# Two 256x256 float32 layers rewritten as three reduced-precision products each, with their tables moved to make room

## The chip, the cores and the metric

The kernel runs on one core of one Trainium2 chip. The metric is the device time of one execution in microseconds (us); three executions of the kernel before gave 1525.33, 1526.73 and 1530.22 us, median 1526.73.

A core has five engines with one in-order queue each: TensorE (PE in the profile; its weight loads are listed as PEld), VectorE (DVE), ScalarE (ACT), GpSimd (POOL) and SyncE (SP, which here only issues DMAs).

## The reference, cut to what matters

The program is a chain of four residual layers on x of shape 4 x 1024 x 256: a linear recurrence with a small network behind it, a sparse feed-forward layer, attention, and the feed-forward layer again. The change touches the first one only:

```python
u = einsum('btd,edh->ebth', x, W_in) + b_in          # three 256x256 layers
in_r, in_i, o = u
h = scan(lam * h + gamma * (in_r + 1j * in_i))        # along the 1024 tokens
out = h.real @ W_mid[0] - h.imag @ W_mid[1] + b_mid[0] - b_mid[1] + o
y = gelu(out @ w1_w + w1_b)                           # first square layer
y = y @ w2_w + w2_b + out                             # second square layer
return layer_norm(y) * ln_g + ln_b                    # added to x
```

The input x is layer-normalized on the way in. The two square layers, 256 x 256 each, are applied to all 4096 tokens.

## The kernel before, in words

**Tiling.** The 4096 tokens lie in 8 blocks of 512; a batch row of 1024 tokens is two blocks, the even and the odd tokens (`CH = 2`), so that one step of the recurrence covers two tokens. Features lie on partitions in two halves of 128 (`KD = 2`, indices `c` for the output half and `k` for the input half). Everything up to about 298 us is this layer plus the heads (normalize, transpose, small convolution) of the feed-forward layer behind it; then come the feed-forward tiles, the attention (the longest stage) and the second feed-forward layer.

**Steps of a block.** `Lru.head` (L357) normalizes and transposes a block of x and splits it into a high and a low part (`xnt`, type float32r). `Lru.states` (L381) makes the inputs of the recurrence on TensorE (tile `pu`), evacuates them on ScalarE (L390), rotates them by tables of cosines and sines `ct`, `st` on VectorE (L402 to L407), scans (L410) and rotates back (L411 to L416). `Lru.outputs` (L422) makes `po` on TensorE (L432 and L437), evacuates it with its bias into `ot` on ScalarE (L438), multiplies by the first square matrix in float32 (L443, tile `pz`), applies Gelu into `zt` (L446), multiplies by the second (L452), adds bias and `ot` on VectorE (L455), transposes (L465), normalizes and adds to x: `yn` on ScalarE (L474), three adds or products on GpSimd (L482 to L484). `Ffn.head` (L501) then takes the finished x.

**Two kinds of product.** The float32 products are single `matmul` calls on float32 tiles. The split products (`products`, L165) take three float32r matmuls for one product of two matrices: high by high, high by low, low by high.

**Tables.** `Lru.tables` (L230) builds `ct` and `st` by doubling, each one tile of 128 x 2 x 512 in the pool of the layer. `Ffn.head` keeps the convolution's output of block b in tiles `xc0` to `xc7` (L507) of the pool `ffn_b`.

**What sets the order.** The body (from L1075) lists the work block by block; a block's `outputs` is followed by the `states` of a later batch row (blocks 2 to 5 only), by the head of a block four further on and by the head of the feed-forward layer two behind. A scheduler then orders each engine's queue by its own timing model, so the queues interleave neighbouring steps; at run time an instruction that waits holds up all that stands behind it on its engine. Two places are pinned by hand: `issue_after(lru.evacuated[7])` (L1095) puts the loads of x blocks 4 to 7 and of the feed-forward weights behind the eighth evacuation of `states` in ScalarE's queue, and the last block is worked in two halves of 256 tokens (L1117). The weights are loaded from ScalarE's queue as well (L215 to L225).

The two calls of the square layers:

```python
            for k in range(KD):
                nc.tensor.matmul(
                    pz, w[:, k, 2, c * P : (c + 1) * P], ot[:, k, :], start=(k == 0), stop=(k == KD - 1)
                )
```

Of the kernel before, what the change touches and what calls it, by code (L numbers as in the profile page):

```python
# [21 lines left out]
P = 128  # L22
# [157 lines left out]
class Banks:  # L180


    def __init__(self, pool, bufs):
        self.pool, self.bufs = pool, bufs
# [10 lines left out]
class Lru:  # L195
# [2 lines left out]

    def __init__(self, tc, ctx, ident, vecs, brow, w_lru, psum):
        self.tc = tc
        nc = self.nc = tc.nc
        self.ident, self.vecs, self.brow, self.psum = ident, vecs, brow, psum
        cp = ctx.enter_context(tc.tile_pool(name="lru_c", bufs=1))
        self.sp = ctx.enter_context(tc.tile_pool(name="lru_s", bufs=2))
        self.wp = ctx.enter_context(tc.tile_pool(name="lru_w", bufs=1))
        self.cp = cp
        self.evacuated, self.scanned, self.xnt_first = [], [], None
        w = self.w = cp.tile([P, KD, 4, D], F32, tag="w", name="w_lru")  # L210
        wt = self.wt = cp.tile([P, KD, 2, D], F32, tag="wt", name="wt")
        self.w_o = cp.tile([P, KD, D], F32, tag="w_o", name="w_o")

        self.w_in, self.w_mid = {0: [], 1: []}, {1: [[w[:, k, e, :] for e in range(2)] for k in range(KD)]}
        for e in range(3):  # L215
            stage = self.w_o if e == 2 else self.sp.tile([P, KD, D], F32, tag="ot", name="stage")
            nc.scalar.dma_start(stage, w_lru[:, :, e])
            parts = self.two(f"w{e}")
            nc.scalar.copy(parts[0], stage)
            nc.gpsimd.tensor_tensor(parts[1], stage, parts[0].bitcast(F32), ALU.subtract)  # L220
            self.w_in[1].append(parts)
            if e == 1:
                nc.scalar.dma_start(wt, w_lru[:, :, 7:9])
        for e in (slice(3, 5), slice(5, 7)):
            nc.scalar.dma_start(w[:, :, e.start - 3 : e.stop - 3], w_lru[:, :, e])  # L225

    def two(self, name):
        return [self.cp.tile([P, KD, D], F32R, tag=f"{name}{i}", name=f"{name}{i}") for i in range(2)]
# [1 line left out]
    def tables(self, between):  # L230
        nc, cp, vecs = self.nc, self.cp, self.vecs
        par = exp_exact(nc, cp, vecs[:, V_PAR : V_PAR + 6], 6, "par")
        nc.scalar.mul(self.w[:, :, 1, :], self.w[:, :, 1, :], -1.0)

        levels = TC.bit_length()
        ang = cp.tile([P, levels, KD], F32, tag="ang", name="ang")
        powers = cp.tile([P, levels, KD], F32, tag="powers", name="powers")
        for l in range(levels):
            nc.gpsimd.memset(powers[:, l, :], float(2**l))
        nc.vector.tensor_tensor(ang, powers, par[:, None, 2:4].to_broadcast([P, levels, KD]), ALU.mult)  # L240
        cn, sn, self.turns = cos_sin(nc, cp, ang.rearrange("p l c -> p (l c)"), levels * KD)
# [12 lines left out]


        ct = self.ct = cp.tile([P, KD, TC], F32, tag="ct", name="ct")
        st = self.st = cp.tile([P, KD, TC], F32, tag="st", name="st")
        nc.gpsimd.memset(ct[:, :, 0:1], 1.0)
        nc.gpsimd.memset(st[:, :, 0:1], 0.0)
        for l in range(levels - 1):  # L260
            n = 2**l
            for c in range(KD):
                t1 = self.wp.tile([P, 512], F32, tag="u0", name="t1", bufs=4)
                t2 = self.wp.tile([P, 512], F32, tag="u1", name="t2", bufs=4)
                c0, s0 = ct[:, c, 0:n], st[:, c, 0:n]
                c1, s1 = ct[:, c, n : 2 * n], st[:, c, n : 2 * n]
                ca, sa = (v[:, (l + 1) * KD + c : (l + 1) * KD + c + 1] for v in (cn, sn))
                if c == 0:
                    nc.vector.tensor_scalar(t1[:, 0:n], s0, sa, None, ALU.mult)
                    nc.vector.tensor_scalar(t2[:, 0:n], c0, sa, None, ALU.mult)  # L270
                else:
                    nc.scalar.mul(t1[:, 0:n], s0, sa)
                    nc.scalar.mul(t2[:, 0:n], c0, sa)
                nc.vector.scalar_tensor_tensor(c1, c0, ca, t1[:, 0:n], ALU.mult, ALU.subtract)
                nc.vector.scalar_tensor_tensor(s1, s0, ca, t2[:, 0:n], ALU.mult, ALU.add)

    def first_weights(self, lam):
# [1 line left out]
        nc, cp, vecs, wt = self.nc, self.cp, self.vecs, self.wt  # L279
        self.turn = [[lam[:, i, k : k + 1] for i in range(2)] for k in range(KD)]  # L280

        tw = [self.sp.tile([P, KD, D], F32, tag="zt", name=f"tw{e}") for e in range(2)]
# [27 lines left out]
    def output_weights(self):  # L310

        nc, cp, vecs, w, wt = self.nc, self.cp, self.vecs, self.w, self.wt
        gw = [self.sp.tile([P, KD, D], F32, tag="zt", name=f"gw{e}") for e in range(2)]
# [67 lines left out]
    def states(self, xnts, c):  # L381
# [11 lines left out]
            self.evacuated.append(last.ins)  # L393
            u.append(ue)
        ur, ui = u
        cc, ss = self.ct[:, c, :], self.st[:, c, :]
# [20 lines left out]
        return full  # L417

    def buffers(self):
        return [self.sp.tile([P, KD, 512], F32, tag=t, name=t, bufs=n) for t, n in (("ot", 2), ("zt", 2))]  # L420

    def outputs(self, r, xs, xnt, h, pairs, last, tag="po", bufs=None):  # L422

# [4 lines left out]
        ot, zt = bufs or self.buffers()  # L428
        for c in range(KD):
            co = slice(c * P, (c + 1) * P)  # L430
            po = self.psum.tile([P, 512], tag, "po")[:, 0:n]
            self.inputs(po, r, 2, c, xnt, sl, stop=False)  # L432
            terms = [
                (self.w_mid[r][k][e][:, co], h[k][e][:, sl.start + r : sl.stop + r]) for k in range(KD) for e in range(2)
            ]
            for i, (lt, v) in enumerate(terms):
                nc.tensor.matmul(po, lt, v, start=False, stop=(i == len(terms) - 1))  # L437
            nc.scalar.activation(ot[:, c, :], po, AF.Identity, bias=self.ob[:, r, c : c + 1])  # L438
            yield
        for c in range(KD):  # L440
            pz = self.psum.tile([P, 512], "pu", "pz")[:, 0:n]
            for k in range(KD):
                nc.tensor.matmul(  # L443
                    pz, w[:, k, 2, c * P : (c + 1) * P], ot[:, k, :], start=(k == 0), stop=(k == KD - 1)
                )
            last_gelu = nc.scalar.activation(zt[:, c, :], pz, AF.Gelu, bias=vecs[:, V_B1 + c : V_B1 + c + 1])  # L446
        self.last_gelu = last_gelu.ins
        yield
        for c in range(KD):
            pz = self.psum.tile([P, 512], tag, "pz2")[:, 0:n]  # L450
            for k in range(KD):
                nc.tensor.matmul(  # L452
                    pz, w[:, k, 3, c * P : (c + 1) * P], zt[:, k, :], start=(k == 0), stop=(k == KD - 1)
                )
            nc.vector.scalar_tensor_tensor(  # L455
                ot[:, c, :], pz, vecs[:, V_B2 + c : V_B2 + c + 1], ot[:, c, :], ALU.add, ALU.add
            )
# [30 lines left out]
class Ffn:  # L488
# [12 lines left out]
    def head(self, blk, sp, psum, ptag, pairs=(0, 1), xtag="fx", ttag="ft"):  # L501
# [17 lines left out]
        for i, j in enumerate(pairs):  # L519
            r = slice(2 * j, 2 * j + 2)  # L520
            xs = self.x[blk * 4 + 2 * j : blk * 4 + 2 * j + 2]
            pt = normalized_t(nc, sp, psum, xtag, ptag, xs, norm[:, 0, r], norm[:, 1, r], w.ident)
            tt = sp.tile([P, KD, 256], F32, tag=ttag, name="ft", bufs=2 if self.dram else 1)
            nc.scalar.copy(tt, pt)  # L524
            yield
            if self.dram:
# [458 lines left out]
def run(*gens):  # L985
    for g in gens:
        for _ in g:
            pass
# [51 lines left out]
def tile_kernel(ctx: ExitStack, tc: tile.TileContext, x_in, w_lru, vecs_in, rows, w_ffn, lin_t, w_attn, w_down, out):  # L1040
# [34 lines left out]
    with ExitStack() as c1:  # L1075
        psum = Banks(c1.enter_context(tc.tile_pool(name="ps1", space=PSUM)), {"pu": 2, "po": 2, "py": 2, "pt": 2})

        brow = c1.enter_context(tc.tile_pool(name="brow", bufs=1)).tile([P, 2, D], F32, tag="brow", name="brow")
        lru = Lru(tc, c1, ident, vecs, brow, w_lru, psum)
# [33 lines left out]
        for blk in range(4, NBLK - 3):  # L1113
            run(f1.head(blk, lru.sp, psum, "pt"))
        k = NBLK - 1
        ot, zt = lru.buffers()
        halves = [  # L1117
            lru.outputs(k % CH, xb[k], xnt[k], h[k // CH], (i,), last, tag, [v[:, :, c : c + 256] for v in (ot, zt)])
            for i, tag, c in ((0, "pu", 0), (1, "po", 256))
        ]  # L1120
        for i in (0, 0, 1):
# [6 lines left out]
        run(*(f1.head(NBLK - 1, lru.sp, psum, "pu", (i,), "lx", "zt") for i in range(2)))  # L1128

    with ExitStack() as c2:  # L1130
        sp = c2.enter_context(tc.tile_pool(name="at_s", bufs=2))
# [193 lines left out]
```

## Time and profile before

| | us |
|---|---|
| median of the runs shown | 1526.73 |
| the profiled execution | 1528.76 |
| its span, first to last instruction | 1527.0 |
| mean granted TensorE clock, share of full speed | 0.946 |
| first product of the recurrence layer (L170) begins | 22.06 |
| first square layer begins (L443, block 0) | 82.91 |
| last square layer's results transposed (L465) | 274.6 |
| feed-forward logits begin (L556) | 297.9 |

How to read the profile: durations are of one profiled execution. In the view of instructions in order of time a row is start, duration, engine, line, operation, output<-input, shape, and how many were merged; brackets hold the idle time of the engine before it and what released it. In the table of windows, the figures are busy us of each engine in that stretch and the granted TensorE clock. A float32 matmul leaves two records, a float32r matmul one. The ends of matmuls are modelled, so the rate is read from the distance between starts: the duration that a record shows is about 0.16 us longer.

Engines in the stages of this layer (busy us of the stretch):

| stretch, us | length | PE | DVE | ACT | POOL | clock |
|---|---|---|---|---|---|---|
| 82.9 to 93.7, block 0 behind the recurrence | 10.8 | 8.71 | 8.55 | 6.73 | 3.26 | 0.86 |
| 94.1 to 116.7, block 1 | 22.6 | 19.57 | 16.29 | 13.44 | 13.07 | 1.00 |
| 116.7 to 142.6, block 2 | 25.9 | 25.81 | 13.24 | 8.85 | 8.34 | 0.94 |
| 142.6 to 170.0, block 3 | 27.4 | 26.07 | 21.91 | 11.31 | 12.85 | 1.00 |
| 170.0 to 199.5, block 4 | 29.5 | 27.26 | 18.88 | 11.89 | 8.36 | 0.94 |
| 199.5 to 226.3, block 5 | 26.8 | 26.80 | 19.09 | 9.72 | 8.36 | 1.00 |
| 226.3 to 254.6, block 6 | 28.3 | 24.10 | 18.39 | 10.52 | 8.33 | 0.94 |
| 254.6 to 274.6, block 7 in halves | 20.0 | 19.65 | 11.64 | 8.35 | 5.57 | 1.00 |

### The profile page before, as it was taken

How to read it: one execution, taken by the hardware profiler on the slowest of the kernel's cores; microseconds unless marked ns; L12 is line 12 of the kernel's file. 1: busy time of each engine (PE TensorE's matmuls, PEld its weight loads, DVE VectorE, ACT ScalarE, POOL GpSimd, SP SyncE). 2: the span in 40 equal slices, each digit the busy share in tenths (PEclk: the TensorE clock that was granted, in tenths of full speed). 3: DMA queues.
4: the chain of work that ended last, by engine and by line, in shares of the span. 5: the costliest groups of instructions: out<-in, count | busy, mean ns of one | idle time of the engine just before them, and what ended most of it. 6: DMA issues, size and time to landing. Idle time of an engine off the chain costs nothing. (4 is left out here: it accounts for less than half of the span.)

```text
span 1527.0 us, 28727 instructions
## 1 busy us (share of the span) xinstructions
PE 1286.5 (84%) x10134; PEld 955.6 (63%) x10136; DVE 1184.6 (78%) x3682; ACT 1017.5 (67%) x2152; POOL 680.3 (45%) x849
## 2 busy tenths in 40 slices
PE   4879998697898898888998989889999999566675
PEld 3535465376677766766776767677777777334454
DVE  8976665697868887878768687777676675599998
ACT  5353433566887877797777787877777776475674
POOL 2033332161545454544544554454344444067776
PEclk9999999698999999999999999999999999688899
DMA  3110000321454343434433445334344545000000
GB/s 118 32 41 15 21 21 21 128 97 49 84 93 90 61 77 73 77 70 82 82 74 60 72 79 86 61 61 83 68 82 79 92 86 96 1 15 24 22 25 28
DMA packets 288609, 96.51 MB, mean 63 GB/s; under 512 B 268233, under 2 KB 284626, under 8 KB 288466
## 3 DMA queue, kind: packets, MB, share of 16 engines
q1 hardware_dynamic: 283024, 88.50, 28.7%
q10 hardware_dynamic: 5442, 6.18, 1.2%
q8 instruction: 80, 1.31, 0.4%
q14 instruction: 63, 0.52, 0.1%
HBM read 16.01 MB, written 11.53 MB: 18 GB/s over the span
## 5 line engine op out<-in xcount | busy, mean ns | idle before, releaser
L898 POOL TENSOR_TENSOR pd<-pr,pd 128x1024 f16<-128x1024 f32 x128 | 273.5, 2141 | 247.6 <-ACT pd L897 185.7
L890 DVE TENSOR_REDUCE nm<-sc 128x1 f32<-128x1024 f32 x256 | 308.5, 1217 | 78.9 <-PE sc L886 77.5
L894 ACT ACTIVATE pr<-sc,nm 128x1024 f32<-128x1024 f32 x256 | 285.9, 1119 | 84.6 <-DVE nm L892 47.0
L886 PE MATMUL sc<-kh,qs 128*128 128x512 f32 x512 | 184.3, 438 | 26.4 <-ACT pr L894 18.8
L886 PE MATMUL sc<-kl,qs 128*128 128x512 f32 x512 | 162.0, 397 | 0.0
L674 DVE MATCH_REPLACE8 wk<-m,wk 128x256 f32<-128x256 f32 x384 | 154.9, 406 | 0.1
L910 ACT COPY p<-ptp 128x512 f32<-128x512 f32 x224 | 124.1, 590 | 45.3 <-PE ptp L905 33.7
L674 DVE MAX8 m<-wk 128x8 f32<-128x256 f32 x384 | 151.3, 412 | 0.4
L930 PE MATMUL pmo<-p,la 128*64 128x128 f32 x2048 | 144.0, 289 | 6.1 <-ACT ft L524 2.9
L905 PE MATMUL ptp<-ident,pr 128*128 128x128 f32 x1024 | 138.3, 275 | 12.9 <-ACT pr L894 12.4
L930 PEld LDWEIGHTS pmo<-p,la 128*64 128x64 f32 x2048 | 122.8, 144 | 25.0 <-ACT ft L524 5.1
L905 PEld LDWEIGHTS ptp<-ident,pr 128*128 128x128 f32 x1024 | 115.6, 140 | 34.8 <-ACT pr L894 22.2
L897 ACT CAST pd<-pr 128x1024 f16<-128x1024 f32 x128 | 133.5, 1054 | 5.6 <-DMA d<-pd 4.6
L886 PEld LDWEIGHTS sc<-kh,qs 128*128 128x128 f32 x512 | 85.2, 195 | 51.1 <-ACT pr L894 29.8
L886 PEld LDWEIGHTS sc<-kl,qs 128*128 128x128 f32 x512 | 97.0, 190 | 23.2 <-issue 1.4
L930 PE MATMUL pmo<-d,lb 128*64 128x128 f16 x3072 | 103.4, 222 | 7.6 <-DVE qs L853 2.6
L930 PEld LDWEIGHTS <-lb 128*64 128x64 f16 x3072 | 92.2, 111 | 26.3 <-issue 20.1
L628 POOL TENSOR_TENSOR ex<-ex,wk 128x512 f32<-128x512 f32 x61 | 77.6, 1273 | 57.4 <-DVE wk L674 45.5
L926 POOL COPY rows<-rs 128x128 f32<-128x128 f32 x128 | 36.1, 294 | 124.4 <-PE pmo L938 76.3
L941 DVE TENSOR_TENSOR on<-pmo,rb 128x128 f32<-128x128 f32 x128 | 36.4, 285 | 66.8 <-ACT rb L940 66.3
L147 PE MATMUL pt<-ident,xn 128*128 128x128 f32 x256 | 47.8, 309 | 44.5 <-ACT xn L145 32.9
L699 PE MATMUL pf<-wf,vt 128*128 128x256 f32 x288 | 81.2, 427 | 4.6 <-ACT vt L697 4.2
(307 smaller groups left out, 2768.6 us busy)
## 6 DMA issues: line engine op xcount, KB each, us to landing
tt<-ft SPq DMA_DIRECT2D x16, 256.0 KB
tt<-tt SPq DMA_DIRECT2D x8, 512.0 KB
out<-x SPq DMA_DIRECT2D x32, 128.0 KB
x<-in_x ACTq DMA_DIRECT2D x6, 512.0 KB
pf<-pfs SPq DMA_DIRECT2D x12, 256.0 KB
full<-pf SPq DMA_DIRECT2D x24, 128.0 KB
d<-pd SPq DMA_TRANSPOSE x128
wa<-in_w_attn SPq DMA_DIRECT2D x2, 640.0 KB
```

Of the source, the lines that this page charges most:

```text
L147: nc.tensor.transpose(pt[:, k, i * P : (i + 1) * P], xn[:, k * P : (k + 1) * P], ident)
L628: pool.tensor_tensor(ex, ex, wk, ALU.subtract)
L674: ins = make(*args).ins
L699: nc.tensor.matmul(dst, vt[:, k, :], w.wf[:, k, :], start=(k == 0 and bias is None), stop=(k == KD - 1))
L886: nc.tensor.matmul(sc[:, sl], qs[:, j, q * P : (q + 1) * P], kk[:, sl], start=(i == 0), stop=(i == 1))
L890: nc.vector.tensor_reduce(nm, sc, AX.X, ALU.max, negate=True)
L894: nc.scalar.activation(pr, sc, AF.Exp, bias=nm, accum_out=ssum[:, j : j + 1])
L897: nc.scalar.copy(pd[:, 0, :], pr)
L898: nc.gpsimd.tensor_tensor(pd[:, 1, :], pr, pd[:, 0, :], ALU.subtract)
L905: nc.tensor.transpose(pt[:, kk, :], pr[:, kc * P : (kc + 1) * P], self.ident)
L910: nc.scalar.copy(dst, pt)
L930: nc.tensor.matmul(po[j * HD : (j + 1) * HD, 0, :], v, pts[j][:, c, :], start=(n == 0), stop=(n == len(terms) - 1),)
```

## The change

- Both square layers take split products. The weights `w1_w` and `w2_w` are loaded to two staging tiles and split once into high and low parts (`w_gelu`), a copy on ScalarE and a subtraction on GpSimd each.
- The data are split per block and half: ScalarE evacuates `po` twice, into `oh` (float32r) and `ot` (float32), and VectorE subtracts to get `ol`. Gelu is taken twice, into `zt` and then `zh`, and VectorE subtracts to get `zl`.
- A new method `square` runs six float32r matmuls where two float32 ones stood: high and low weights by the high data for both `k`, then the high weights by the low data.
- To make room, the tables become four tiles that lie in the space of `xc4` to `xc7`; `w_o` lies in `xc0`, the two staging tiles in `xc1` and `xc2`. `zt` goes from two buffers to one; `oh`, `ol`, `zh`, `zl` have one each. Users of the second `zt` buffer (`tw`, `gw`, the last feed-forward heads) take `ot`, `oh` or `ol`.

The diff, cut to its core:

```diff
+        tables = [bp.tile([P, TC], F32, tag=f"xc{NBLK - 4 + i}", name=f"table{i}") for i in range(4)]
+        self.ct, self.st = tables[0:KD], tables[KD:]
...
-        w = self.w = cp.tile([P, KD, 4, D], F32, tag="w", name="w_lru")
+        w = self.w = cp.tile([P, KD, 2, D], F32, tag="w", name="w_lru")
...
+        self.w_gelu = [self.two(f"g{e}") for e in range(2)]
+        for e in range(2):
+            stage = bp.tile([P, KD * D], F32, tag=f"xc{1 + e}", name="stage").rearrange("p (k d) -> p k d", k=KD)
+            nc.scalar.dma_start(stage, w_lru[:, :, 5 + e])
+            high, low = self.w_gelu[e]
+            nc.scalar.copy(high, stage)
+            nc.gpsimd.tensor_tensor(low, stage, high.bitcast(F32), ALU.subtract)
...
+    def square(self, dst, e, c, v):
+
+        wh, wl = (t[:, :, c * P : (c + 1) * P] for t in self.w_gelu[e])
+        terms = [(t[:, k, :], v[0][:, k, :]) for k in range(KD) for t in (wh, wl)]
+        terms += [(wh[:, k, :], v[1][:, k, :]) for k in range(KD)]
+        for i, (x, y) in enumerate(terms):
+            self.nc.tensor.matmul(dst, x, y, start=i == 0, stop=i == len(terms) - 1)
...
-            nc.scalar.activation(ot[:, c, :], po, AF.Identity, bias=self.ob[:, r, c : c + 1])
+            for v in (oh, ot):
+                nc.scalar.activation(v[:, c, :], po, AF.Identity, bias=self.ob[:, r, c : c + 1])
+            nc.vector.tensor_tensor(ol[:, c, :], ot[:, c, :], oh[:, c, :].bitcast(F32), ALU.subtract)
...
-            for k in range(KD):
-                nc.tensor.matmul(
-                    pz, w[:, k, 2, c * P : (c + 1) * P], ot[:, k, :], start=(k == 0), stop=(k == KD - 1)
-                )
-            last_gelu = nc.scalar.activation(zt[:, c, :], pz, AF.Gelu, bias=vecs[:, V_B1 + c : V_B1 + c + 1])
+            self.square(pz, 0, c, (oh, ol))
+            for v in (zt, zh):
+                last_gelu = nc.scalar.activation(v[:, c, :], pz, AF.Gelu, bias=vecs[:, V_B1 + c : V_B1 + c + 1])
+            nc.vector.tensor_tensor(zl[:, c, :], zt[:, c, :], zh[:, c, :].bitcast(F32), ALU.subtract)
...
-            for k in range(KD):
-                nc.tensor.matmul(
-                    pz, w[:, k, 3, c * P : (c + 1) * P], zt[:, k, :], start=(k == 0), stop=(k == KD - 1)
-                )
+            self.square(pz, 1, c, (zh, zl))
```

More of the change, by code (lines that the diff above doesn't have):

```diff
@@ L195, with __init__ @@
 class Lru:
-    def __init__(self, tc, ctx, ident, vecs, brow, w_lru, psum):
+    def __init__(self, tc, ctx, ident, vecs, brow, w_lru, psum, bp):
         self.tc = tc
@@ L209, in __init__ @@
         self.evacuated, self.scanned, self.xnt_first = [], [], None
-        w = self.w = cp.tile([P, KD, 4, D], F32, tag="w", name="w_lru")
+        w = self.w = cp.tile([P, KD, 2, D], F32, tag="w", name="w_lru")
         wt = self.wt = cp.tile([P, KD, 2, D], F32, tag="wt", name="wt")
-        self.w_o = cp.tile([P, KD, D], F32, tag="w_o", name="w_o")
+        self.w_o = bp.tile([P, KD * D], F32, tag="xc0", name="w_o").rearrange("p (k d) -> p k d", k=KD)
         self.w_in, self.w_mid = {0: [], 1: []}, {1: [[w[:, k, e, :] for e in range(2)] for k in range(KD)]}
         for e in range(3):
-            stage = self.w_o if e == 2 else self.sp.tile([P, KD, D], F32, tag="ot", name="stage")
+            stage = self.w_o if e == 2 else self.sp.tile([P, KD, D], F32, tag="ot", name="stage", bufs=2)
             nc.scalar.dma_start(stage, w_lru[:, :, e])
@@ L223, in __init__ @@
                 nc.scalar.dma_start(wt, w_lru[:, :, 7:9])
-        for e in (slice(3, 5), slice(5, 7)):
-            nc.scalar.dma_start(w[:, :, e.start - 3 : e.stop - 3], w_lru[:, :, e])
+        nc.scalar.dma_start(w, w_lru[:, :, 3:5])
+        self.w_gelu = [self.two(f"g{e}") for e in range(2)]
[5 more added lines that the diff above has]
+            nc.gpsimd.tensor_tensor(low, stage, high.bitcast(F32), ALU.subtract)
     def two(self, name):
@@ L253, in tables @@
         between()
[L256 to L259, printed above, removed]
+        ct, st = self.ct, self.st
+        for c in range(KD):
+            nc.gpsimd.memset(ct[c][:, 0:1], 1.0)
+            nc.gpsimd.memset(st[c][:, 0:1], 0.0)
         for l in range(levels - 1):
@@ L264, in tables @@
                 t2 = self.wp.tile([P, 512], F32, tag="u1", name="t2", bufs=4)
-                c0, s0 = ct[:, c, 0:n], st[:, c, 0:n]
-                c1, s1 = ct[:, c, n : 2 * n], st[:, c, n : 2 * n]
+                c0, s0 = ct[c][:, 0:n], st[c][:, 0:n]
+                c1, s1 = ct[c][:, n : 2 * n], st[c][:, n : 2 * n]
                 ca, sa = (v[:, (l + 1) * KD + c : (l + 1) * KD + c + 1] for v in (cn, sn))
@@ L280, in first_weights @@
         self.turn = [[lam[:, i, k : k + 1] for i in range(2)] for k in range(KD)]
-        tw = [self.sp.tile([P, KD, D], F32, tag="zt", name=f"tw{e}") for e in range(2)]
+        tw = [self.sp.tile([P, KD, D], F32, tag=t, name="tw", bufs=b) for t, b in (("zt", 1), ("ot", 2))]
         for k in range(KD):
@@ L312, in output_weights @@
         nc, cp, vecs, w, wt = self.nc, self.cp, self.vecs, self.w, self.wt
-        gw = [self.sp.tile([P, KD, D], F32, tag="zt", name=f"gw{e}") for e in range(2)]
+        gw = [self.sp.tile([P, KD, D], F32, tag=t, name="gw", bufs=b) for t, b in (("zt", 1), ("ot", 2))]
         for e in range(2):
@@ L395, in states @@
         ur, ui = u
[L396 removed]
+        cc, ss = self.ct[c][:, :], self.st[c][:, :]
         full = [wp.tile([P, TC + 1], F32, tag=f"h{e}{c}", name=f"h{e}{c}", bufs=2) for e in range(2)]
@@ L419, in buffers @@
     def buffers(self):
-        return [self.sp.tile([P, KD, 512], F32, tag=t, name=t, bufs=n) for t, n in (("ot", 2), ("zt", 2))]
+        return [
+            self.sp.tile([P, KD, 512], dt, tag=t, name=t, bufs=n)
+            for t, n, dt in (("ot", 2, F32), ("zt", 1, F32), ("oh", 1, F32R), ("ol", 1, F32R), ("zh", 1, F32R), ("zl", 1, F32R))
+        ]
+    def square(self, dst, e, c, v):
[4 more added lines that the diff above has]
+            self.nc.tensor.matmul(dst, x, y, start=i == 0, stop=i == len(terms) - 1)
     def outputs(self, r, xs, xnt, h, pairs, last, tag="po", bufs=None):
@@ L427, in outputs @@
         n = len(tiles) * P
-        ot, zt = bufs or self.buffers()
+        ot, zt, oh, ol, zh, zl = bufs or self.buffers()
         for c in range(KD):
@@ L522, in head @@
             pt = normalized_t(nc, sp, psum, xtag, ptag, xs, norm[:, 0, r], norm[:, 1, r], w.ident)
-            tt = sp.tile([P, KD, 256], F32, tag=ttag, name="ft", bufs=2 if self.dram else 1)
+            tt = sp.tile([P, KD, 256], F32, tag=ttag, name="ft", bufs=2 if self.dram and ttag == "ft" else 1)
             nc.scalar.copy(tt, pt)
@@ L1078, in tile_kernel @@
         brow = c1.enter_context(tc.tile_pool(name="brow", bufs=1)).tile([P, 2, D], F32, tag="brow", name="brow")
-        lru = Lru(tc, c1, ident, vecs, brow, w_lru, psum)
+        lru = Lru(tc, c1, ident, vecs, brow, w_lru, psum, bp)
         xb = [x[4 * k : 4 * k + 4] for k in range(NBLK)]
@@ L1115, in tile_kernel @@
         k = NBLK - 1
-        ot, zt = lru.buffers()
+        whole = lru.buffers()
         halves = [
-            lru.outputs(k % CH, xb[k], xnt[k], h[k // CH], (i,), last, tag, [v[:, :, c : c + 256] for v in (ot, zt)])
+            lru.outputs(k % CH, xb[k], xnt[k], h[k // CH], (i,), last, tag, [v[:, :, c : c + 256] for v in whole])
             for i, tag, c in ((0, "pu", 0), (1, "po", 256))
@@ L1127, in tile_kernel @@
             run(f1.head(NBLK - 2, lru.sp, psum, "pt"))
-        run(*(f1.head(NBLK - 1, lru.sp, psum, "pu", (i,), "lx", "zt") for i in range(2)))
+        run(*(f1.head(NBLK - 1, lru.sp, psum, "pu", (i,), "lx", ("oh", "ol")[i]) for i in range(2)))
     with ExitStack() as c2:
```

## The prediction

> **What bounds the kernel now.** I read the busy shares first, then TensorE's idle time by releaser inside the recurrence layer, then the rows around each square layer.
>
> ```profile
> PE 1286.5 (84%) x10134; PEld 955.6 (63%) x10136; DVE 1184.6 (78%) x3682; ACT 1017.5 (67%) x2152; POOL 680.3 (45%) x849
> ```
>
> The share over the whole span decides nothing here: the change is in the stretch from 82.9 us (first square layer) to 274.6 us (last transposes). There TensorE is busy 178.4 of 192.1 us, VectorE 128.7, ScalarE 81.2. So TensorE bounds this stretch, and its idle time is the following (from 82.9 us on; the 8.2 us lie just ahead of the stretch):
>
> ```profile
> PE pz L443 <- ACT ot L438: 8.2, 1, 8.2
> PE po L437 <- DVE norm_f L66: 4.2, 1, 4.2
> PE pz L452 <- ACT zt L446: 3.4, 2, 2.1
> PE py L465 <- DVE ot L455: 3.2, 2, 3.0
> PE po L437 <- DVE norm_f L136: 1.6, 1, 1.6
> PE pc L529 <- ACT ft L524: 0.7, 1, 0.7
> ```
>
> Some 13 us of waits in the stretch. Each is a point where TensorE's clock is reset by another engine: time saved ahead of it on TensorE alone is lost there. The 4.2 us (at 238.4, block 6) and 1.6 us (about 176, block 4) end with VectorE, whose queue holds the scans of the second batch rows; the 3.0 us (116.7, block 1) end with L455 behind a normalization chain on VectorE; 2.1 us (90.1, block 0) and 1.3 us (160.8, block 3) end with Gelu.
>
> **What leaves TensorE.** The rows of block 3:
>
> ```profile
> 155.41 3.60 PE L443 MATMUL pz<-ot,w_lru 128*128 128x512 f32 x8
> ...
> 160.77 1.98 PE L452 MATMUL pz<-zt,w_lru 128*128 128x512 f32 x4 [1.32 <-ACT zt L446]
> 162.19 1.96 PE L170 MATMUL pu<-xnt,w 128*128 128x512 f32 x6
> 163.99 1.56 PE L170 MATMUL pu<-xnt,f 128*128 128x512 f32 x6
> 165.39 1.02 PE L452 MATMUL pz<-zt,w_lru 128*128 128x512 f32 x2
> ```
>
> Eight float32 records take (3.60 - 0.16) / 8 = 0.43 us each, so a half layer (one c, two matmuls, four records) takes 1.72. Six float32r records of the same width take 165.39 - 163.99 = 1.40, 0.233 each. The edit puts six of these in place of four of those: 0.32 us saved per half layer. Blocks 0 to 6 have 28 half layers: 9.0 us. Block 7 works 256 columns: its float32 half layer takes 4 x 0.216 = 0.87, six float32r records at 0.134 take 0.81, and eight of these save 0.4. Together TensorE loses 9.4 us of work. Bounds: where the type changes, a first group of six spans 1.80 (162.19 to 163.99), which would cost 0.08 per half layer, 2.2 us in all; but the start of such a group overlaps the float32 record ahead of it (160.77 + 1.72 is 162.49), so I take 1.40. The Trainium skill (FP8 and Floating Point Precision, "TensorE Precision Notes") says that true float32 makes four passes through the array. Three products for four passes would be 1.29 in place of 1.72, 12.0 us for the 28; the row gives 9.0, because a float32r pass takes 0.233 here and not 0.215. The row is taken.
>
> **What it adds on ScalarE and VectorE.** Evacuation and Gelu are done twice: 28 more of 128x512 at 0.69 (L438, L446; some 0.6 from start to start) and 8 of 128x256 at 0.47, 23 us. VectorE gets 28 subtractions 128x512 at 0.67 (L412's row) and 8 at about 0.35, 21.6 us. Spread over seven blocks of some 27 us this is 3 us per block on either engine. Both have idle time for it (VectorE 63 us, ScalarE 111 us of the 192). What counts is which of it stands ahead of something TensorE needs:
>
> - First layer. The copy to `oh` comes first and is ready when `ot` was before. The low part comes 0.6 + 0.67 later, but its products come last: eight products with high data (1.87 us) cover that. Nothing, where ScalarE and VectorE are free.
> - Second layer. ScalarE runs zt, zh, zt, zh; the second zh comes 0.6 us after the point at which the second zt came, in the best case. In blocks 2 to 5 the products for `pu` lie between high and low terms in the built order and cover it; in blocks 0, 1, 6 and 7 only four or eight products do. If ScalarE holds other work (three `yn` at 158.67 just ahead of zt), the wait grows.
> - Behind the last low part: `zl` stands in VectorE's in-order queue and waits for `zh`. Behind it queue whatever the order has put there: the normalization chains (some 3 us) and L455, for which the transposes (L465) wait.
>
> **Where these fall, block by block** (shift of the changed kernel against before, positive is later, from the rows' durations in the built order):
>
> - Head: two weight copies on ScalarE (0.57 each) and two subtractions on GpSimd (L220's row, 1.26), and one `ol` ahead of VectorE's last scans, whose queue is full until 82 us: +1.1. The weight bytes are the same, from the same queue (one load split in three, two issues more at 0.43); they land before they are needed at 82 us. SyncE's queue is unchanged. The pinned loads keep their place.
> - Block 0. ScalarE is blocked by its own DMA issues here:
>
> ```profile
> 77.16 4.96 ACTq L1030 DMA_DIRECT2D v<-in_rows  x3
> 82.17 1.26 ACT L438 ACTIVATE ot<-po,ob 128x512 f32<-128x512 f32 x2 [9.20 <-DMA wf<-in_w_ffn]
> ...
> 89.41 1.26 ACT L446 ACTIVATE zt<-pz,vecs 128x512 f32<-128x512 f32 x2
> ```
>
>  zh of half 1 starts about 91.5 in place of zt's 90.0. The subtractions then wait in VectorE's queue, and L455 with its transposes comes at about 97.3 where it came at 94.1: +3.2, although TensorE has 1.3 less to do.
> - Block 1 ends with VectorE (the 3.0 us wait): no gain, +3.5. Block 2: TensorE is busy 25.8 of 25.9 us before, so its 1.28 is gained, and given back to a wait of about 1.4 for the first zh: +3. Block 3: the old 1.32 wait goes (its `yn` now stand behind zt and zh), and the products gain: +0.8.
> - Block 4 waits for VectorE's scans anyway, which now have two subtractions and later statistics among them: +2.2. Block 5: TensorE again the bound, -1.3 and some waits: about +0.5 to its end. Block 6 again waits at L437 for the scans (4.2 us before): +1. Block 6's own products give -0.7: about +0.3. Block 7 in halves: neutral, +0.5 at the last transposes (274.6 before).
>
> Behind 275 us the built order is the same but for some attention-weight products among the feed-forward tiles at 290 to 350; their cost I bound by -2 and +2 and take nothing, since the same instructions run there.
>
> **Tables and buffers.** They sit in `xc4` to `xc7`, first written again by a feed-forward head after the last scan; the stages sit in `xc1`, `xc2`, free long before. One `zt` buffer: the next block's Gelu comes some 20 us after the last read. I cost these at nothing; the distance of 20 us is the cover. If it were gone, the wait would be one half block of TensorE work, some 10 us, once.
>
> **A rule against the change.** The Trainium skill (SBUF — State Buffer, "Who interferes with whom") says that a VectorE instruction with two inputs in SBUF and a GpSimd instruction that reads SBUF exclude each other. The 36 subtractions are of that kind. The trace shows it:
>
> ```profile
> 98.04 0.16 DVE L65 TENSOR_TENSOR lx_t<-lx_t,lx_v 128x4 f32<-128x4 f32 x1
> ...
> 110.41 0.65 DVE L65 TENSOR_TENSOR lx_t<-lx_t,lx_v 128x4 f32<-128x4 f32 x1
> ```
>
> In the second row GpSimd ran L482 to L484 back to back, 0.74 each. By the rule each of the 28 could wait up to 0.74, 21 us on VectorE; by L412's row alone none. GpSimd is busy 68 of 192 us, so about a third of 28 meet one: 28 x 0.35 x 0.5 = 5 us on VectorE (an estimate), of which I put 0.5 us on TensorE's path, because only the waits in blocks 0, 1, 4 and 6 end with VectorE. What else meets: GpSimd's adds to x would be late by as much.
>
> **The sum.** +0.5 at 275 us, +0.5 for the ports: span 1528.0 in place of 1527.0, execution 1529.8 in place of 1528.8. The median of the runs is 2.0 below that execution: 1527.7.
>
> **The rivals** (0.3%, 4.6 us, is about what a measurement of this kernel can tell from no change).
>
> - A, 1527.7, chance 0.46: TensorE's 9.4 us are absorbed by waits for zh, zl and the scans. For it: the resets at blocks 0, 1, 4 and 6. Against: ends of block 2, 3 and 5 have TensorE as the only bound. Its own range, from the block sums' uncertainty of some 4 us: 1523.5 to 1531.5.
> - B, 1519.3, chance 0.17: TensorE stays the bound all along: the low terms and `pu` products cover ScalarE and VectorE. -9.4 + 2.0 for the head and block 0. For it: 93% TensorE. Against: the six waits above.
> - C, 1534, chance 0.32, slower: zt, zh, zt, zh run one behind the other on ScalarE, behind `yn` and `xn` that stand there, and zl behind them on VectorE; TensorE waits at the second layer of each block for four activations and a subtraction, 4 x 0.6 + 0.2 left uncovered = 2.6, against 1.28 saved: 7 x (2.6 - 1.28) = +9.2, less the 1.6 that block 4's wait takes up: +7.6. It decides from the point at which the wait per block is over 1.28 us.
> - D, 1533, chance 0.05: the split products run at the 0.30 us per record of the first group, so nothing is saved: +1.0 + 2.2, and half of A's 9.4, some 3 to 4 us of which the path now misses in blocks 2, 3 and 5.
>
> Slower by over 0.3% (above 1531.3): C, most of D: 0.35. Faster (below 1522.1): B, 0.17. Within: 0.48. The range, 1518 to 1536, takes in A, B's and C's centres.
>
> **What would show it.** In the changed profile: records of the new `square` 0.233 apart (D is wrong), TensorE's waits for `zh` and `zl` in place of `zt`; transposes of block 0 at about 97.3; waits at L437's successor for VectorE still there in blocks 4 and 6; last transposes near 275 and the logits near 298 us. Waits for `zh` and `zl` of under 4 us in all would show B, of over 14 us C. Subtractions with a mean over 0.75 would show the ports dearer than taken. The prediction is wrong if the scheduler's new order makes a reset of its own that I took for covered, above all behind VectorE's scans, or if the later stages move by more than 2 us.

## The result and the profile after

The changed kernel took 1551.26 us (median of six executions, 1545.99 to 1553.56), beside 1530.26 us for the kernel before in its six (the three shown and three of the same session): ratio 1.0139, 95% interval 1.0122 to 1.0156. It is slower by 21 us. A second session gave 1549.09 beside 1529.71, ratio 1.0125, interval 1.0103 to 1.0147. The prediction said 1527.7 with a range up to 1536.

The first line of the profile after has the instruction counts that the edit should give (36 more on VectorE); its span is 1548.6 us:

```profile
PE 1293.0 (83%) x10208; PEld 974.6 (63%) x10208; DVE 1205.4 (78%) x3718; ACT 1037.9 (67%) x2190; POOL 693.1 (45%) x853
```

TensorE's busy time over the whole span tells as little as before. Where the 21 us came from is read at points that both kernels pass. The first transposes of a block (L465 before, L484 after) mark its end; the score products are the first matmuls of the attention. Two profiles of each kernel (the second ones are from the experiments below; us from the start of the span):

| point | before | before again | after | after again | mean shift |
|---|---|---|---|---|---|
| first transposes of block 0 | 94.1 | 95.4 | 100.3 | 98.7 | +4.7 |
| block 1 | 116.7 | 117.9 | 125.7 | 124.1 | +7.6 |
| block 2 | 143.7 | 145.0 | 151.5 | 149.9 | +6.4 |
| block 3 | 170.3 | 171.7 | 179.7 | 178.1 | +7.9 |
| block 4 | 201.5 | 203.0 | 211.9 | 210.3 | +8.9 |
| block 5 | 226.9 | 228.4 | 236.3 | 234.7 | +7.9 |
| block 6 | 258.2 | 260.7 | 269.9 | 268.1 | +9.6 |
| last transposes | 274.3 | 276.9 | 286.2 | 284.4 | +9.7 |
| first score product of the attention | 376.0 | 378.0 | 387.7 | 388.6 | +11.2 |
| last score product | 1292.0 | 1294.5 | 1314.1 | 1313.6 | +20.6 |
| end of the span | 1527.0 | 1529.6 | 1548.6 | 1548.8 | +20.4 |

So there are two losses of about the same size: 10 us in the recurrence layer, where the change is, and 9 us in the attention stage, which it does not touch.

The first loss, split into TensorE's work and its idle time up to the last transposes, before and after (from left: stretch, length, busy us and records of PE, then of PEld, DVE, ACT, POOL; the third figure from the end is the granted clock):

```profile
0.00:274.60 274.60, 229.51 (x856) 140.61 (x856) 205.66 (x722) 115.86 (x222) 78.16 (x155) 0.96 0.12 38
0.00:286.50 286.50, 227.89 (x928) 153.59 (x928) 226.95 (x750) 135.28 (x260) 89.79 (x159) 0.95 0.11 37
```

In the mean of the two profiles of each kernel, TensorE's busy time fell by 4.0 us (231.7 to 227.7) and its idle time grew by 13.7.

TensorE's waits in the recurrence layer after the change (releaser; us in total, times, longest):

```profile
PE pz L441 <- ACT oh L460: 7.9, 1, 7.9
PE pz L441 <- ACT zh L467: 6.4, 5, 3.5
PE po L458 <- DVE ly_t L64: 5.6, 1, 5.6
PE po L458 <- DVE fx_t L64: 4.5, 1, 4.5
PE py L484 <- DVE ot L474: 3.1, 3, 1.5
PE pz L441 <- DVE zl L468: 2.0, 2, 1.5
PE pz L441 <- DVE ol L461: 1.1, 1, 1.1
PE pt L147 <- DVE xnt L161: 1.0, 1, 1.0
```

L441 is the new `square`, L458 the old L437, L484 the old L465. The 3.4 us for zt became 6.4 for zh, and 3.1 for the low parts came on top. The two waits for VectorE ahead of L458 (blocks 4 and 6) grew from 1.6 to 4.5 and from 4.2 to 5.6. The first line differs from before: there both halves of block 0's first layer waited, here only the products with the second half of oh do.

At full clock the products run about as fast as was worked out. Block 4:

```profile
197.81 2.10 PE L441 MATMUL pz<-oh,g 128*128 128x512 f32 x8
199.75 1.10 PE L441 MATMUL pz<-ol,g 128*128 128x512 f32 x4
```

Eight records in 199.75 - 197.81 = 1.94 us, 0.243 each, where 0.233 was taken: the first of them, behind products of another type, takes 0.31 and the others 0.23. In block 0 they run at half clock, behind its two waits:

```profile
86.49 1.22 PE L441 MATMUL pz<-oh,g 128*128 128x512 f32 x2 [7.95 <-ACT oh L460]
...
93.80 2.87 PE L441 MATMUL pz<-zh,g 128*128 128x512 f32 x6 [3.53 <-ACT zh L467]
96.47 0.63 PE L441 MATMUL pz<-zl,g 128*128 128x512 f32 x1
```

Six records take 96.47 - 93.80 = 2.67 us here, 0.445 each. Summed over the records up to the last transposes, half clock lengthened TensorE's work by 12.0 us after the change and by 9.7 before (means of two profiles each; the two of the kernel before differ by 3 us). Without that, the work fell by some 6.4 us.

### The profile page after: what moved, and what is told of

Read it like the earlier page. It is cut to its first block, busy times and chain, and to the rows that moved or that the text cites. A ratio compares the mean times of both kernels' runs of the same rounds, so it can differ in the third digit from the quotient of the medians.

```text
span 1548.6 us, 28951 instructions
## 1 busy us (share of the span) xinstructions
PE 1293.0 (83%) x10208; PEld 974.6 (63%) x10208; DVE 1205.4 (78%) x3718; ACT 1037.9 (67%) x2190; POOL 693.1 (45%) x853
## 5 line engine op out<-in xcount | busy, mean ns | idle before, releaser
L913 ACT ACTIVATE pr<-sc,nm 128x1024 f32<-128x1024 f32 x256 | 286.2, 1121 | 88.2 <-DVE nm L911 55.8
L905 PEld LDWEIGHTS sc<-kh,qs 128*128 128x128 f32 x512 | 85.8, 197 | 54.8 <-ACT pr L913 32.8
```

What stands on the lines that cost most here:

```text
L905: nc.tensor.matmul(sc[:, sl], qs[:, j, q * P : (q + 1) * P], kk[:, sl], start=(i == 0), stop=(i == 1))
L913: nc.scalar.activation(pr, sc, AF.Exp, bias=nm, accum_out=ssum[:, j : j + 1])
```

## The experiments

Theory S: TensorE waits for the serial pairs on ScalarE and the subtractions on VectorE. Rivals: the layout (L), the added work in the queues whoever reads it (Q), the float32r products themselves (P). Times are medians with the ratio to runs of the kernel before on the same chip. In every run the scheduler could order all queues anew: a difference of two runs holds the edit and the new order together. Positions are from one profile each; the two profiles of one kernel differ by up to 2.6 us. The number to watch is the last transposes, 275.6 before (mean of 274.3 and 276.9) and 285.3 after.

**The control**, no edit.

> The kernel before, unchanged, profiled once more as a control for the attention stage, whose instructions the change does not touch. From the first to the last score product (sc) the kernel before took 915.3 us and the changed kernel 925.7 us. If that stage's length belongs to a kernel (theory W: something in the changed kernel's later stages differs for good), this run has 914 to 917 us. If it is only what one execution happened to meet in throttled clock and late transposing DMAs (rival V), it can lie anywhere from 913 to 926. Time: ratio 1.000.

1528.07 us, ratio 0.9994 (0.9979 to 1.0009); attention 916.5 us, as in the first profile.

**Layout alone.**

```diff
-            self.square(pz, 0, c, (oh, ol))
+            (two float32 matmuls, as before; the same for the second layer)
-            for v in (oh, ot):
+            for v in (ot,):
-            nc.vector.tensor_tensor(ol[:, c, :], ...)
```

> The changed kernel with float32 products in both square layers and no second evacuations and subtractions: only the moved tables, the single zt buffer and the moved staging tiles are left. Theory S (serial copies on ScalarE and subtractions on VectorE stand ahead of TensorE): ratio 0.998 to 1.003, first square layer's second half near 83 us, last transposes at 274 to 276. Rival L (the layout and the buffers cost): 1.004 to 1.010.

1527.23 us, ratio 0.9979 (0.9962 to 0.9996); last transposes at 269.0. Neither theory had that: 6.6 us earlier than before. The trace shows a part of why. In ScalarE's queue both evacuations of block 0's `po` (67.97 and 69.69) now stand ahead of the DMA issues; before they stood behind them, at 82.17. But block 0 gains only 2.2 us. By block 2 it is 6.5 (137.8 beside 144.4 in the mean before): the 3.0 us wait for L455 in block 1 is down to 1.0, and the six float32r records behind it take 1.64 us where they took 2.91 before.

**Added work that nobody reads.**

```diff
-            self.square(pz, 0, c, (oh, ol))
+            (two float32 matmuls on ot, zt; oh, ol, zh, zl are still made)
```

> The changed kernel with float32 products in both square layers, but oh, ol, zh, zl are still made; nothing reads them. Work that nothing waits for. Theory S in its strict form (TensorE waits for the low and high parts): the waits are gone, so 1.000 to 1.005, last transposes 274 to 280. Rival Q (the added work delays what else is queued on ScalarE and VectorE, whoever reads it): 1.007 to 1.014, last transposes at 283 or later.

1534.96 us, ratio 1.0037 (1.0025 to 1.0049); last transposes at 280.0, 11.0 later than with the layout alone. That is at S's upper end and three us short of Q's: the work costs 11 us by standing in the queues. L455's successor is waited for 6.4 us in all, where the kernel before waited 3.2.

**Six products, of the added work only the copies to oh.**

```diff
-        terms += [(wh[:, k, :], v[1][:, k, :]) for k in range(KD)]
+        terms += [(wh[:, k, :], v[0][:, k, :]) for k in range(KD)]
-            for v in (zt, zh):
+            for v in (zh,):
-            nc.vector.tensor_tensor(zl[:, c, :], ...)   (and ol)
```

> The changed kernel without low parts of the data: Gelu is taken once, into zh; no subtractions; the third pair of products reads the high data, so six float32r products remain (the low data's contribution is left out). The oh copy stays. Theory S and rival Q both: TensorE's saving shows, last transposes at 266 to 273, ratio 0.993 to 0.999 if the attention stage keeps 915 us. Rival P (float32r products themselves cost, by clock or rate): last transposes at 277 or later, 1.003 or more.

1529.7 us, ratio 0.9997 (0.9981 to 1.0012), but the last transposes are at 260.5: 8.5 us earlier than the layout alone, and 5.5 earlier than both theories said. TensorE's saving is real, P falls. And the total did not move, since the attention stage of this profile took 931.2 us. That was the sign that the second loss is a matter of its own.

**Added work, six products, no wait for low parts.**

```diff
-        terms += [(wh[:, k, :], v[1][:, k, :]) for k in range(KD)]
+        terms += [(wh[:, k, :], v[0][:, k, :]) for k in range(KD)]
```

> The changed kernel with every copy and subtraction kept, six float32r products per half layer, but the last pair reads the high data again (the low data's contribution is left out), so TensorE never waits for ol and zl. Last transposes: before 274.3 and 276.9 in two profiles, changed kernel 286.2, float32 products with the added work 280.0, six products without it 260.5. Theory S (TensorE waits for the low parts): most of the loss goes, 270 to 275. Rival Q (the added work in the queues costs, whoever reads it; the products' gain is lost in other waits): 279 or later.

1527.74 us, ratio 0.9994 (0.9982 to 1.0007); last transposes at 269.8, as S said, against 285.3 for the changed kernel. All the added instructions are there; what went is TensorE's need of ol and zl, and with it the place that they and others got in the order. So of the 15.5 us, not all is waiting for low parts: 5.5 are TensorE's own busy time (222.2 us up to the last transposes, 227.7 in the changed kernel, 3.4 of it by half clock), the other 10 are idle time. Its waits of the same kind:

```profile
PE pz L441 <- ACT zh L467: 2.7, 4, 0.9
PE py L484 <- DVE ot L474: 1.9, 2, 1.1
```

**One layer alone.** First only, then second only (the other layer as in the layout run).

> Only the first square layer takes split products; the second is float32, with one Gelu. Its ol has 1.87 us of cover in the high products. Theory S: last transposes at 265 to 270 (the layout alone gives 269.0). Rival Q: half of the added work, 274 to 278. Time, with the throttle as in the layout run: S 1522 to 1528, Q 1531 to 1536.

> Only the second square layer takes split products; Gelu twice, one subtraction. Theory S, with the serial zt, zh, zt, zh as the seat of the loss: nearly the whole loss, last transposes 279 to 286, time 1538 to 1549. Rival Q: half of it, 274 to 278.

First only: 1530.38 us, ratio 1.0007 (0.9986 to 1.0027), last transposes at 270.9. Second only: 1536.97, ratio 1.0052 (1.0037 to 1.0067), 274.9. Over the layout's 269.0 these are +1.9 and +5.9; both together are +16.3. So the second layer costs more, as the chain Gelu, Gelu, subtraction says, but not nearly the whole loss: e6 lies where rival Q had it, and e5 just outside S's range. Half of the loss is there only when both layers are split. That their pairs then meet in the two queues is my reading; no run shows it apart from the order.

**Subtractions on GpSimd.**

```diff
-            nc.vector.tensor_tensor(ol[:, c, :], ot[:, c, :], oh...
+            nc.gpsimd.tensor_tensor(ol[:, c, :], ot[:, c, :], oh...   (and zl)
```

> The changed kernel with its 36 data subtractions on GpSimd in place of VectorE, 1.26 us each in place of 0.67. If VectorE's in-order queue (subtractions that wait for zh ahead of normalization and L474) is the seat: last transposes 274 to 280, time 1535 to 1542. If the length of the chain Gelu, Gelu, subtraction is: 0.6 us more for each low part, 287 to 296, time 1551 or more.

1562.11 us, ratio 1.0210 (1.0186 to 1.0234), last transposes at 302.5. Freeing VectorE's queue was no help; the longer way to the low part (1.60 us for ol and 1.29 for zl, where 0.70 and 0.77 were) was 17 us dearer, beyond the range that I gave. Of the 17, 6 are half clock: it lengthened TensorE's work by 18.0 us here, by 12.0 in the changed kernel.

**Three repairs**, each on the changed kernel, then all together.

```diff
 e8   -  nc.vector.tensor_tensor(ol, ot, oh, subtract)
      +  nc.vector.scalar_tensor_tensor(ol, po, bias, oh, add, subtract)
 e9   -  per half: zt, zh          +  zh, zh, then zt, zt
 e10  -  with tc.issue_after(lru.evacuated[7]):
      +  with tc.issue_after(lru.last_po):     (block 0's last evacuation of po)
```

> The changed kernel, but ol is made in one VectorE instruction from PSUM (po plus bias minus oh), so it waits for one evacuation and not for two: the first layer's low part comes about 0.6 us earlier per half. The last transposes of the changed kernel are at 286.2. Theory S1 (the first layer's chain oh, ot, ol is part of the loss): 279 to 283, time 1541 to 1547. Rival S2 (the loss sits in the second layer and in block 0's DMA issues): 285 to 287, time 1548 to 1552.

> The changed kernel with the Gelus in the order zh, zh, zt, zt over the two halves in place of zt, zh, zt, zh: the second zh comes 1.2 us earlier, the low parts when they came before or 0.6 later for the first half. Theory S2 (the wait for the second zh is what TensorE loses): waits for zh from 6.4 to under 3 us, last transposes 280 to 283. Rival S3 (the low parts zl and what queues behind them on VectorE set the end): 285 to 289.

> The changed kernel with the loads of x blocks 4 to 7 and of the feed-forward weights pinned behind block 0's last evacuation of po in ScalarE's queue, in place of behind the eighth evacuation of states: the second half of oh no longer stands behind 10 us of DMA issues. If that is what block 0 loses (theory B0): its first transposes at 93 to 95 in place of 100.3, last transposes 278 to 281, time 1541 to 1545. Rival (the later resets take it up, or x of block 4 lands late): last transposes 284 to 288.

> All three edits together: ol from PSUM, zh, zh, zt, zt, and the loads behind block 0's evacuations. Theory S with its parts added: last transposes 268 to 275, time 1527 to 1537. Rival (the parts overlap, VectorE's scans in blocks 4 and 6 set the end): 277 to 282, time 1538 to 1545.

| run | us, ratio (interval) | block 0 | last transposes |
|---|---|---|---|
| e8 | 1546.6, 1.0099 (1.0081 to 1.0116) | 98.6 | 287.0 |
| e9 | 1542.5, 1.0084 (1.0062 to 1.0107) | 97.7 | 279.2 |
| e10 | 1542.2, 1.0066 (1.0044 to 1.0088) | 95.0 | 278.2 |
| e11 | 1538.05, 1.0046 (1.0028 to 1.0064) | 93.4 | 276.3 |

e8 decides nothing: its last transposes are where S2 had them, its time is where S1 had it, and in its profile half clock lengthened TensorE's work by 16.0 us, 4 more than in the changed kernel. e9: the new order of the Gelus is worth 6 us (waits for zh 6.4 to 3.5, where I had said under 3). e10: the new place of the loads is worth 7. Together they give 9, not 13, between the two ranges given for e11; it reaches the time of before in this layer, still 7 behind the layout alone. What e10 moves is seen in ScalarE's rows. The changed kernel, where oh of half 1 stands behind the issues:

```profile
81.52 4.18 ACTq L1049 DMA_DIRECT2D v<-in_rows  x3
85.75 0.69 ACT L460 ACTIVATE oh<-po,ob 128x512 fp32r<-128x512 f32 x1 [9.04 <-DMA wf<-in_w_ffn]
86.34 0.68 ACT L460 ACTIVATE ot<-po,ob 128x512 f32<-128x512 f32 x1
86.95 0.41 ACT L1050 CAST linb<-v 128x256 bf16<-128x256 f32 x1
88.95 0.81 ACT L1053 CAST linb<-v 32x256 bf16<-32x256 f32 x2 [1.60 <-POOL v L1051]
90.77 0.40 ACT L1055 CAST linb<-v 32x256 bf16<-32x256 f32 x1 [1.00 <-POOL v L1054]
91.19 1.28 ACT L467 ACT_TABLE_LOAD   x1
...
92.48 0.69 ACT L467 ACTIVATE zt<-pz,vecs 128x512 f32<-128x512 f32 x1
```

and e10, where it stands ahead of them, and zt of half 0 starts 4 us earlier:

```profile
77.45 0.69 ACT L460 ACTIVATE oh<-po,ob 128x512 fp32r<-128x512 f32 x1 [0.94 <-PE po L458]
...
82.45 4.76 ACTq L1050 DMA_DIRECT2D v<-in_rows  x3
87.24 1.28 ACT L468 ACT_TABLE_LOAD   x1 [8.52 <-DMA lint<-in_lin_t]
88.53 0.69 ACT L468 ACTIVATE zt<-pz,vecs 128x512 f32<-128x512 f32 x1
```

But the edit moved more than the issues. In the changed kernel, as in the one before, four casts of feed-forward weights (L1050 to L1055), with 2.6 us of waits for GpSimd, stand between the last evacuation and the first Gelu; in e10 they stand behind the Gelus. In e4 oh of half 1 stands behind the issues as well (85.07), but only one cast stands ahead of the first zt (87.94), and block 0's first transposes come at 93.4, earlier than in e10. So e10's gain in block 0 cannot be put down to the place of oh alone.

**The second loss.** Three runs for the attention stage and the layout's gain.

> The changed kernel, unchanged, profiled and timed again. Time 1548 to 1553, ratio 1.012 to 1.016, mean clock 0.933 to 0.937 over the executions, last transposes 285 to 287. Theory W (the lower clock in the attention stage belongs to this kernel): attention stage 923 to 929 us. Rival V (one execution's luck): 915 to 920.

> The kernel before with 26 copies of the last feed-forward input onto itself on ScalarE, a pure delay of 8 to 12 us between the recurrence layer and the feed-forward tiles. If the later start alone lowers the clock (rival D): attention stage 920 to 927 us, mean clock 0.935 to 0.939, time 1543 to 1551. If not: 914 to 918 us, clock 0.942 to 0.945, time 1536 to 1541.

> The kernel before with the loads of x blocks 4 to 7 and of the feed-forward weights pinned behind block 0's last evacuation of po. If the order of ScalarE's queue is what the layout run gained by: last transposes 267 to 271 (before 274.3 and 276.9), time 1520 to 1528. If it is the tables' place or the single zt buffer: 274 to 277, time 1526 to 1531.

e12: 1549.09 us, attention 925.0 us (926.4 in the first profile): the longer stage belongs to this kernel, theory W. e13: 1563.37 us, ratio 1.0216 (1.0192 to 1.0241). My copies also went into the second feed-forward layer, so the tail behind the attention grew by 15 us as well; the run is a poor test of the time. Its attention stage is 919.8 us and lies just short of what rival D said, so it stays inconclusive. e14: last transposes at 269.9, as in the layout run: moving those loads is enough for the layout's gain, and the tables' place and the single zt buffer are not what gave it. Which of the instructions that the scheduler then moved gives it was not separated. But its time is 1531.71, ratio 1.0021 (1.0008 to 1.0034), with 927.8 us for an attention stage whose instructions nobody touched. I had expected 1520 to 1528.

The clock explains a part of this. Time lost to the clock, span times (1 - mean granted clock), over all executions of a kernel:

| kernel | executions | mean clock | lost, us |
|---|---|---|---|
| before (two sessions) | 90 | 0.944 | 85.8 |
| layout | 22 | 0.939 | 92.9 |
| added work | 18 | 0.941 | 91.2 |
| six products | 14 | 0.938 | 94.9 |
| e14 | 22 | 0.937 | 96.3 |
| after (both sessions) | 10 | 0.936 | 99.2 |

In the layout kernel alone the clock of an execution ran from 0.930 to 0.948, and the time with it from 1536.75 to 1517.27 us. Over the executions of all kernels, each taken against the mean of its own, a us lost goes with 0.50 us of time. By that rate the 13.4 us more that the changed kernel loses are 7 of its 20 us. In the attention stage it can be read from TensorE's work on the same records, before and after:

```profile
376.00:1292.00 916.00, 822.39 (x8245) 655.14 (x8246) 687.13 (x1714) 700.90 (x1366) 428.76 (x420) 0.98 0.42 77
387.70:1314.10 926.40, 827.83 (x8245) 659.76 (x8246) 687.13 (x1714) 702.43 (x1366) 429.37 (x420) 0.97 0.44 77
```

In the mean of two profiles each, TensorE is busy 4.5 us longer there, at a lower clock, and idle 5.0 us longer.

Where the clock goes down is seen in the records. In six profiles (both kernels twice, layout, e14) the granted clock changes only at points that lie a multiple of 3.413 us apart. Cut along these points, the attention stage shows what stands ahead of a half-speed stretch. Of the windows at full speed in which TensorE was busy for under 1.7 us, 35 of 40 were followed by half speed; from 1.7 to 2.24 us, 23 of 163; above that, none of 1330. The same gap in both kernels, before (row by row: start, duration):

```profile
594.62 0.63 PE L147 MATMUL pt<-ident,xn 128*128 128x128 f32 x4 [1.84 <-DVE qs L853]
595.47 1.09 PE L905 MATMUL ptp<-ident,pr 128*128 128x128 f32 x8 [0.23 <-ACT pr L894]
```

and after:

```profile
605.79 1.00 PE L147 MATMUL pt<-ident,xn 128*128 128x128 f32 x4 [1.83 <-DVE qs L872]
606.65 1.97 PE L924 MATMUL ptp<-ident,pr 128*128 128x128 f32 x8
```

with the granted clock of that stretch, two windows before the change and two after (columns as above):

```profile
591.07:594.48 3.41, 1.71 (x7) 0.84 (x5) 3.37 (x10) 3.36 (x7) 0.98 (x1) 1.00 0.00 0
594.48:597.90 3.42, 2.94 (x25) 2.27 (x27) 2.90 (x7) 3.42 (x8) 3.42 (x3) 1.00 0.33 64
602.45:605.86 3.41, 1.57 (x7) 0.78 (x6) 3.35 (x10) 3.36 (x7) 1.17 (x1) 1.00 0.01 2
605.86:609.27 3.41, 3.41 (x15) 2.97 (x16) 2.79 (x7) 3.30 (x7) 3.41 (x3) 0.50 0.40 76
```

The wait is the same, 1.83 and 1.84 us, and so is the work. After the change the next 3.41 us ran at half clock and the eight transposes took 1.97 in place of 1.09 us; before the change the clock stayed. The Trainium skill (TensorE: Matmul & The Clock Gate, "Part 1: The HAM clock gate (the "warmup" mystery)") has a free-running activity window of 3.41 us; our stretches have that length. So a gap counts in one kernel and not in the other by how it lies against the window: the window that holds it had 1.71 us of work before and 1.57 after. The counts show this as a rule of thumb; no run moved a gap on purpose, and why the changed kernel meets more such windows stays open. Of the 5.0 us more of idle time in the attention stage, some 3 are waits for the transposing DMAs (`d<-pd`): 5.2 and 5.1 us in the two profiles after, 1.9 and 2.2 before.

## Why the prediction was wrong, step by step

The prediction's sum had two terms that failed. In the layer it let the 9.4 us saved be eaten up by waits, so some 10 us of them, +0.5 in all; measured were 4.0 saved and 13.7 of new idle time, +9.7. Behind the layer it put nothing; measured were 10.7 more.

- **TensorE's saving** (9.4 us predicted): right for the products by themselves, not for the changed kernel. From the run with added work and float32 products to the one with added work and six products without low waits, the last transposes come 10.2 us earlier (280.0 to 269.8) and TensorE's busy time up to there falls by 9.1 (231.3 to 222.2). In the changed kernel it falls by 4.0: about 2.4 us went to half clock, for which the prediction had no term. The rest I read as low products that stand apart from the high ones, so that the slower first record comes more often; that was not tested. Rival D falls. The estimate from four passes was 12. (In the sum for block 7, eight times 0.06 is 0.5 and not 0.4.)
- **The added work** ("Nothing, where ScalarE and VectorE are free"; 0.6 us at the second layer in the best case): failed. It costs 11.0 us by itself (269.0 to 280.0), and the need for the low parts 15.5 more (269.8 to 285.3). With the saving of 10.2 and the layout's 6.6: -6.6 + 11.0 - 10.2 + 15.5 = +9.7, the shift in the table. The sum closes because each term starts where another ends. The terms are differences of kernels whose order and clock differ too, so they say what each need costs with its order, not what one instruction costs.
- **Block by block**: I gave +3.2, +3.5, +3, +0.8 and a return to +0.5; measured +4.7, +7.6, +6.4, +7.9 and never a return. Two of the steps named the right wait and the wrong size. In block 0 the eighth evacuation of `states`, behind which ScalarE issues the loads, came 2.7 us late (mean of two profiles) where the head was put at +1.1; zh of half 1 started at 94.21 where 91.5 was put; and the products behind it ran at half clock. In block 1 I looked only at what queues behind the subtraction; here a chain of normalization stood ahead of it, each step slowed (0.65 us, where the prediction shows 0.16), and the subtraction itself took 1.29 us:

```profile
116.93 0.66 DVE L65 TENSOR_TENSOR lx_t<-lx_t,lx_v 128x4 f32<-128x4 f32 x1
117.63 0.66 DVE L66 SCALAR_TENSOR_TENSOR lx_rs<-lx_t,lx_rs 128x4 f32<-128x4 f32 x1
118.32 0.65 DVE L64 SCALAR_TENSOR_TENSOR lx_t<-lx_rs 128x4 f32<-128x4 f32 x1
118.89 1.29 DVE L468 TENSOR_TENSOR zl<-zt,zh 128x512 fp32r<-128x512 f32 x1
```

 GpSimd worked without a pause beside them:

```profile
118.21 1.43 POOL L503 TENSOR_TENSOR x<-x,yn 128x256 f32<-128x256 f32 x2
```

 zt and zh of that half had ended by 116.8; TensorE got zl at 120.24. The third, block 3 (-2.2 predicted from block 2 to 3), failed in direction: the old wait for zt did not go, it became waits for ol (1.1) and zh (0.7).
- **The scans in blocks 4 and 6** (later by the two subtractions ahead of them): the waits came where they were expected and grew by 2.9 and 1.4 us. They did not give back the earlier shift: behind them block 4 is 8.9 us late and block 6 9.6. VectorE was as late as TensorE. That is where A's argument broke: a wait gives lost time back only if the engine that ends it is not delayed by the same change.
- **The ports** (5 us on VectorE, 0.5 on the path): the means are 0.70 for ol and 0.77 for zl where 0.67 was alone, 14 x 0.03 + 14 x 0.10 = 1.8 us; the eight of half the width took 0.49 where 0.35 was taken, 1.1 us more. Some 3 us in all, less than taken; but one of them was the row above, on the path.
- **Tables and buffers** (nothing): their place cost nothing: with it (layout, 269.0) and without it (e14, 269.9) the layer ends within a us. But the new order gained 6.6 us in the layout run, and in the full change that gain was gone. The weights come in three loads where two were, so one issue more and not two; this changes nothing.
- **Behind 275 us** ("the same instructions run there", -2 to +2): failed. The attention's instructions took 9 us longer, about half of it as longer work at the lower clock and a third as waits for late DMAs. The prediction named this as a way to be wrong (later stages that move by more than 2 us), but gave it no cost.
- **Rival C** came nearest in the number: its +7.6 us is close to the layer's +9.7. Its mechanism is there only in part. It took 2.6 us of waits in each of seven blocks, and the prediction's own sign for it was waits for zh and zl of over 14 us; they were 8.4, and more than half of the zh part was block 0's 3.5. So the nearness is partly luck; and C had no term for the stages behind either.

The layout kernel is the only one whose interval lies below the kernel before, 0.9979 (0.9962 to 0.9996). None with split products in both layers and both low parts came below it.

## What to carry to other kernels

A copy that splits a value in two costs its duration once on the engine that makes it, but the consumer pays for the whole chain behind it and for all that stands in the in-order queues around it: here 9 us of matmul time were to be gained, 4 were, and 14 us of idle time came with them. An in-order queue holds other work as well, and a new order can put it ahead of what the bounding engine needs: look at everything between two dependent rows, not only at the rows of the change. A wait that ends with another engine hides lost time only if the change leaves that engine alone. And where a whole stage behind the edit runs on the edge of TensorE's clock, count its loss with the gaps: compare mean granted clock over many executions before taking a gain of some microseconds for real.

## What the runs showed that was not expected

- One kernel's time follows its mean clock: 1517 us at 0.948, 1537 us at 0.930, over 22 executions of one program.
- The clock of the attention stage goes window by window: a window of 3.413 us with under 1.7 us of TensorE's work nearly always had half speed behind it, one with over 2.24 never had, in the six profiles counted.
- All kernels of the table that were changed have a lower mean clock (0.936 to 0.941) than the kernel before (0.944), those with float32 products in both square layers and no other work too. Why the unedited order is the best of them for the clock is open; no run settles it.
- e3 gained 15 us in the recurrence layer and nothing in the end: in its profile the attention stage, which nobody edited, gave all of it back.
